# Adding the last expert layer's rows to the result in the scattering DMA, with the tiles beyond 28 in a branch

## The chip, the cores and the metric

The kernel runs on one core of one Trainium2 chip. The time is that of the device for one execution, in microseconds (us); lower is better. An execution was also recorded by the hardware profiler; its times are counted from the start of its span. PE is the matrix engine, DVE the vector engine, ACT the activation engine, POOL the GpSimd engine, SP the engine that issues most DMAs.

## The reference, cut to what matters

A graph network of two layers on 3125 nodes of 256 features. Each layer adds a graph convolution and an attention block to the stream `x`, then a mixture of experts. Only the last step, the experts of the second layer, matters here (`D` is 256, `H` 512, eight experts, two of them for each node):

```python
    mu = jnp.mean(x, axis=-1, keepdims=True)
    var = jnp.mean(jnp.square(x - mu), axis=-1, keepdims=True)
    xn = (x - mu) * jax.lax.rsqrt(var + EPS) * gamma + beta
    logits = jnp.einsum('bsd,de->bse', xn, Wr) + br
    top_vals, top_idx = jax.lax.top_k(logits, K)
    w = jax.nn.softmax(top_vals, axis=-1)
    w_full = jnp.einsum('bsk,bske->bse', w, jax.nn.one_hot(top_idx, E, dtype=w.dtype))
    y = jnp.zeros(x.shape[:-1] + (DOUT,), x.dtype)
    for e in range(E):
        h = jax.nn.gelu(jnp.einsum('bsd,dh->bsh', xn, W1[e]) + b1[e], approximate=False)
        y_e = jnp.einsum('bsh,hd->bsd', h, W2[e]) + b2[e]
        y = y + y_e * w_full[..., e, None]
    return y
```

The result is `x` plus this `y`: for each node, the stream before the step, plus two experts' outputs weighted by their gates.

## The kernel before

The stream lives in SBUF as `xs`, 25 tiles of 128 rows (the last of 53), and is worked on in seven groups of four tiles (the seventh is one tile). A framework orders the instructions of each engine and places semaphore waits where one instruction reads or overwrites what another wrote, in SBUF and in DRAM alike; `tc.declare_no_dep` takes such a wait away.

*Routing.* The second graph convolution ends in `sums` (L1271): for one group after another, PE multiplies the 25 row blocks of the adjacency matrix, loaded by SP as `chb` into four buffers, into PSUM. When a group is summed, `done2` (L1520) runs its two dense layers, adds to `xs` (L1543) and calls `route(g)` (L1197). The router normalizes the rows, chooses two experts for each node and gives each choice a place in the expert's list; POOL writes the row, with node number, first expert and both gates behind it, to that place of the DRAM array `slots` by an indirect DMA (L1242). Last, it adds the experts' second bias, weighted by the gates, to `xs` (L1254, L1255). SP's queue runs in order, so what stands in it between loads of `chb` is issued between them. The first five groups have passes of their own; the last two share one.

*The expert tiles.* An expert's list is cut into tiles of 256 rows. Their number depends on the data: at most NST = 32 for 6250 choices. A small table, computed on DVE, names list position and expert of each of the 32 tiles (L1562 to L1587). The loop at L1603 runs all 32, also where the lists fill fewer; the rest read blank rows. A tile: SP reads two numbers from the table and loads the expert's weights (`w1`, `w2`, 512 KB each, three buffers) and 256 rows (`xr`, 260 KB); PE transposes the rows (L190, evacuated at L192), multiplies them by `w1` (L224), ACT applies the gelu (L227), PE multiplies by `w2` (L1633) in two halves of 128 rows, DVE scales each half by its gate into `yo` (L1634, three buffers), and POOL scatters it by row into the DRAM array `y2_d` (L1635; the profile writes `y_d`). All these scatters are declared free of each other.

`y2_d` has a place for each node's first expert and, `HALF` = 3200 rows later, one for its second; rows of `xr` that hold no node go to places of their own behind, which nobody reads. So four operations on DVE make the destination `dest`:

```python
            V.tensor_scalar(second, xr[:, :, D + 1], te[:, i:i + 1], None, op0=OP.not_equal)
            V.scalar_tensor_tensor(unused, xr[:, :, D], float(2 * HALF), lost[:, i, :], op0=OP.is_ge, op1=OP.mult)
            V.tensor_tensor(unused, unused, xr[:, :, D], op=OP.add)
            V.scalar_tensor_tensor(dest, second, float(HALF), unused, op0=OP.mult, op1=OP.add)
```

*The end.* For each of the seven groups SP loads both halves of `y2_d` (L1648, L1651; 512 KB each, four buffers), DVE adds them to `xs` (L1653), and SP stores the group to `out` (L210, L212).

*Elsewhere.* Adding indirect DMAs (`compute_op=OP.add`, L384) build two count matrices in the first half of the kernel, one 4-byte value per partition. Two optional blocks, `residue`, stand in branches (`if_more`, L1324, entered at L1459 and L1514) that aren't entered with these inputs.

Of the kernel before, what the change touches and what calls it, by code (L numbers as in the profile page):

```python
# [8 lines left out]
F32 = mybir.dt.float32  # L9
BF16 = mybir.dt.bfloat16  # L10
I32 = mybir.dt.int32
AF = mybir.ActivationFunctionType
OP = mybir.AluOpType
# [4 lines left out]
P = 128  # L18
N = 3125
D = 256  # L20
NT = 25
NG = 7
LAST = N - 24 * P
NN = N * N
EX = 8
SLOT = 256
CAP = 13 * SLOT
NST = (2 * N + EX * (SLOT - 1)) // SLOT
XW = D + 4
HALF = 25 * P  # L30
E0 = 100000
E1 = 65536
MID = 13 * P
# [18 lines left out]
def rows_of(t):  # L52
    return P if t < NT - 1 else LAST


def tiles_of(g):
    return list(range(4 * g, min(4 * g + 4, NT)))
# [25 lines left out]
def tile_gps(ctx: ExitStack, tc: tile.TileContext, a, out):  # L83
    nc = tc.nc
# [45 lines left out]
    pq_d = dram.tile([9, N], F32, name="pq_d")  # L130
    y_d = dram.tile([NT, P, 4, D], F32, name="y_d")
    slots = dram.tile([EX * CAP + SLOT, XW], F32, name="slots")
    y2_d = dram.tile([3 * HALF + NST * SLOT + P, D], F32, name="y2_d")
    hT_d = dram.tile([P, 4, N], F32, name="hT_d")
    AT2 = AT[0:NN].rearrange("(r c) -> r c", c=N)
    A12 = A1[0:NN].rearrange("(r c) -> r c", c=N)
# [148 lines left out]
    def split_rows(r):  # L285

        return [(0, r)] if r % 16 == 0 else [(0, r - r % 16), (r - r % 16, r)]
# [152 lines left out]
    with ExitStack() as st:  # L440
# [74 lines left out]
        for g in range(NG):  # L515
            ts = tiles_of(g)
# [661 lines left out]
    def router(ps, moe):  # L1178
# [18 lines left out]
        def route(g):  # L1197

            ts = tiles_of(g)
            r, k = rows_of(ts[-1]), len(ts)  # L1200
            rb = moe.tile([P, 4, XW], F32, name="rb", tag="rb", bufs=2)
            nx = [rb[:r, j, :D] for j in range(k)]
            normed(nx, [xs[:r, t, :] for t in ts], r)
            normed(nx, nx, r)
            hT = work.tile([P, 2, 512], F32, name="hT", tag="hT")
            transposed(ps, hT, nx, r, [fcol("gamma", c) for c in range(2)], [fcol("beta", c) for c in range(2)], tag="mm", bufs=3)
            pl = ps.tile([P, 512], F32, name="mm", tag="mm", bufs=3)
            for j, t in enumerate(ts):
                for c in range(2):
                    T.matmul(pl[:r, EX * j:EX * j + EX], lhsT=hT[:, c, j * P:j * P + r], rhs=wr[:, c, :],  # L1210
                             start=(c == 0), stop=False)
                add_bias(pl[:r, EX * j:EX * j + EX], r, br)
            sc = moe.tile([P, 4, EX], F32, name="r_sc", tag="r_sc", bufs=2)
            V.tensor_copy(sc[:r, :k, :], pl[:r, :EX * k].rearrange("p (t e) -> p t e", e=EX))
            gt, rank = gates(moe, sc, EX, "r", nt=k, r=r, bufs=2)

            sel, pos, oh = (moe.tile([P, 4, EX], F32, name=f"r_{nm}", tag=f"r_{nm}", bufs=2)[:r, :k]
                            for nm in ("sel", "pos", "oh"))
            V.tensor_scalar(sel, rank, 1.5, None, op0=OP.is_lt)
            pp = ps.tile([P, 512], F32, name="mm", tag="mm", bufs=3)  # L1220
            sf = sel.rearrange("p t e -> p (t e)")
            T.matmul(pp[:r, :EX * k], lhsT=tri[:r, :r], rhs=sf, start=True, stop=True)
            T.matmul(pp[:, 64:64 + EX * k], lhsT=ones[:r, :], rhs=sf, start=True, stop=True)
            for j in range(k):
                V.tensor_tensor(pos[:, j, :], pp[:r, EX * j:EX * j + EX], nxt[:r], op=OP.add)
                V.tensor_tensor(nxt, nxt, pp[:, 64 + EX * j:64 + EX * j + EX], op=OP.add)
            at = moe.tile([P, 4, 2], F32, name="r_at", tag="r_at", bufs=2)
            ati = moe.tile([P, 4, 2], I32, name="r_ati", tag="r_ati", bufs=2)
            V.tensor_copy(rb[:r, :k, D], node[:r, ts[0]:ts[-1] + 1])
            for i in range(2):  # L1230
                V.tensor_scalar(oh, rank, float(i), None, op0=OP.is_equal)
                V.tensor_tensor(sel, oh, pos, op=OP.mult)
                V.tensor_reduce(at[:r, :k, i], sel, axis=AX.X, op=OP.add)
                V.tensor_tensor(sel, oh, gt, op=OP.mult)
                V.tensor_reduce(rb[:r, :k, D + 2 + i], sel, axis=AX.X, op=OP.add)  # L1235
                if i == 0:
                    V.tensor_tensor(sel, oh, ei[:r, None, :].to_broadcast([r, k, EX]), op=OP.mult)
                    V.tensor_reduce(rb[:r, :k, D + 1], sel, axis=AX.X, op=OP.add)
            V.tensor_copy(ati[:r, :k], at[:r, :k])
            for j in range(k):  # L1240
                for i in range(2):
                    d = G.indirect_dma_start(out=slots, out_offset=bass.IndirectOffsetOnAxis(ap=ati[:r, j, i:i + 1], axis=0),  # L1242
                                             in_=rb[:r, j, :], in_offset=None)
                    for o in spread:
                        tc.declare_no_dep(d.ins, o.ins, reason="every place is given once")
                    spread.append(d)

            for j, t in enumerate(ts):
                p = ps.tile([P, 512], F32, name="mm", tag="mm", bufs=3)
                T.transpose(p[:EX, :r], gt[:, j, :], ident[:r, :r])  # L1250
                gT = moe.tile([EX, P], F32, name="r_gT", tag="r_gT", bufs=2)
                S.activation(gT[:, :r], p[:EX, :r], AF.Copy)
                po = ps.tile([P, 512], F32, name="mm", tag="mm", bufs=3)
                T.matmul(po[:r, :D], lhsT=gT[:, :r], rhs=b2, start=True, stop=True)  # L1254
                V.tensor_tensor(xs[:r, t, :], xs[:r, t, :], po[:r, :D], op=OP.add)  # L1255

        return route

# [290 lines left out]
    with ExitStack() as st:  # L1549
# [3 lines left out]
        def stile(shape, name, dt=F32):  # L1553
            return fp.tile(shape, dt, name=name, tag=name)
# [39 lines left out]
        for h in range(4):  # L1594
            V.tensor_tensor(past, tmp, bb[:, h, :][:, None, :].to_broadcast([P, NST, EX]), op=OP.mult)
            V.tensor_reduce(b1[:, :, h], past, axis=AX.X, op=OP.add)


        lost = stile([P, NST, 2], "t_lost")
        G.iota(lost, pattern=[[SLOT, NST], [P, 2]], base=0, channel_multiplier=0, allow_small_or_imprecise_dtypes=True)  # L1600
        done = []
        why = "computed from counts, clamped above"
        for i in range(NST):  # L1603
            ro = nc.values_load(table[0:1, i, 0:1], engines=[mybir.EngineType.SP], min_val=0, max_val=EX * CAP,
                                skip_runtime_bounds_check_because=why)
            re = nc.values_load(table[0:1, i, 1:2], engines=[mybir.EngineType.SP], min_val=0, max_val=EX - 1,
# [7 lines left out]
            second = fp.tile([P, 2], F32, name="second", tag="second", bufs=3)  # L1614
            gate = fp.tile([P, 2], F32, name="gate", tag="gate", bufs=3)
            dest = fp.tile([P, 2], I32, name="dest", tag="dest", bufs=3)
            V.tensor_scalar(second, xr[:, :, D + 1], te[:, i:i + 1], None, op0=OP.not_equal)
            unused = fp.tile([P, 2], F32, name="unused", tag="unused", bufs=3)
            V.scalar_tensor_tensor(unused, xr[:, :, D], float(2 * HALF), lost[:, i, :], op0=OP.is_ge, op1=OP.mult)
            V.tensor_tensor(unused, unused, xr[:, :, D], op=OP.add)  # L1620
            V.scalar_tensor_tensor(dest, second, float(HALF), unused, op0=OP.mult, op1=OP.add)
            V.tensor_tensor(gate, xr[:, :, D + 3], xr[:, :, D + 2], op=OP.subtract)
            V.tensor_tensor(gate, gate, second, op=OP.mult)
            V.tensor_tensor(gate, gate, xr[:, :, D + 2], op=OP.add)
# [5 lines left out]
            for c in range(2):  # L1630
                po = ps.tile([P, D], F32, name="o", tag="o", bufs=3)
                for h in range(4):
                    T.matmul(po, lhsT=hid[h][:, c * P:(c + 1) * P], rhs=w2[:, h, :], start=(h == 0), stop=(h == 3))  # L1633
                V.tensor_scalar(yo[:, c, :], po, gate[:, c:c + 1], None, op0=OP.mult)  # L1634
                d = G.indirect_dma_start(out=y2_d, out_offset=bass.IndirectOffsetOnAxis(ap=dest[:, c:c + 1], axis=0),  # L1635
                                         in_=yo[:, c, :], in_offset=None)
                for o in done:
                    tc.declare_no_dep(d.ins, o.ins, reason="every result has a place; the dump is not read")
                done.append(d)

        for g in range(NG):
            ts = tiles_of(g)
            r = rows_of(ts[-1])
            for i in range(2):
                y = fp.tile([P, 4, D], F32, name="y2", tag="y2", bufs=4)
                at = HALF * i + 512 * g
                if len(ts) == 4:
                    nc.sync.dma_start(y, y2_d[at:at + 512, :].rearrange("(t p) d -> p t d", p=P))  # L1648
                else:
                    for q0, q1 in split_rows(r):  # L1650
                        nc.sync.dma_start(y[q0:q1, 0, :], y2_d[at + q0:at + q1, :])  # L1651
                xg = xs[:r, ts[0]:ts[-1] + 1, :]
                V.tensor_tensor(xg, xg, y[:r, :len(ts), :], op=OP.add)  # L1653
            store_rows(out, xs[:, ts[0]:ts[-1] + 1, :], g)


# [77 lines left out]
```

## Time and profile before

| | us |
|---|---|
| median of three runs | 5253.3 |
| the three runs | 5243.11, 5253.3, 5254.21 |
| the profiled execution | 5248.96 |
| span of its profile | 5247.1 |
| PE busy in the span | 4047.3 (77%) |
| DVE busy | 3311.5 (63%) |
| POOL busy | 2749.7 (52%) |
| ACT busy | 1361.2 (26%) |

The page cuts the span into 40 equal slices of 131 us; each digit is the busy share in tenths, 9 being 90% or more:

```profile
PE   0456878769666868859879946676799989999596
POOL 0568888888888888877740028788300120010121
DMA  9954543444322222266565554453543221121266
```

Up to slice 21 POOL is busy with the adding scatters of L384 nearly all the time; from slice 30 on, PE is. The expert stage is the last two slices and a little more. Its groups, from the answer by lines for 4600 to 5250 us (busy time, mean ns of one, idle time of the engine ahead of them and what ended it):

```profile
L224 PE MATMUL mm<-xT,f1w 128*128 128x256 f32 x512 | 127.8, 393 | 0.9 <-ACT xT L192 0.8
L1633 PE MATMUL o<-f1w,hid 128*128 128x256 f32 x512 | 115.7, 379 | 0.0
L1635 POOL DMA_INDIRECT y_d<-yo,dest x64 | 62.0, 968 | 199.1 <-DVE yo L1634 176.4 <-DVE gate L1622 22.5 <-issue 0.3
L1634 DVE TENSOR_SCALAR yo<-o,gate 128x256 f32<-128x256 f32 x64 | 30.9, 483 | 57.3 <-PE o L1633 56.5
L1653 DVE TENSOR_TENSOR xs<-xs,y 128x1024 f32<-128x1024 f32 (+1 forms) x14 | 15.5, 1109 | 22.0 <-DMA y<-y_d 22.0
```

### The profile page before, as it was taken

What the parts mean: (1) busy time and instruction counts of PE and PEld (TensorE: products, weight loads), DVE (VectorE), ACT (ScalarE), POOL (GpSimd) and SP (SyncE); (2) the same over time, 40 slices, a digit from 0 to 9 for tenths busy, and PEclk for the clock granted to TensorE, in tenths of its full rate; (3) what the DMA queues carried; (4) which work ended last, traced back from release to release, by engine and by line L of the source; (5) the groups of instructions that cost most, each with busy time, mean ns of one, the idle gap of its engine ahead of it and who ended that gap; (6) DMA issues with size and microseconds to landing.
All of it is one profiled execution on the core that took longest, in us unless ns stands there. A gap on an engine that the chain in (4) does not pass through costs nothing. (4 is left out here: it accounts for less than half of the span.)

```text
span 5247.1 us, 49144 instructions
## 1 busy us (share of the span) xinstructions
PE 4047.3 (77%) x16209; PEld 2337.5 (45%) x16277; DVE 3311.5 (63%) x8366; ACT 1361.2 (26%) x2089; POOL 2749.7 (52%) x1869
## 2 busy tenths in 40 slices
PE   0456878769666868859879946676799989999596
PEld 0244445445434554524456622232354444545485
DVE  7979887898799985123459978889860222321422
ACT  0111122113111211100025459898420120000132
POOL 0568888888888888877740028788300120010121
PEclk9867887889778878879989967688899999999798
DMA  9954543444322222266565554453543221121266
GB/s 355 332 131 72 83 63 53 78 79 61 25 17 25 25 17 8 5 137 128 89 184 203 180 142 124 116 140 93 182 126 89 65 80 52 53 59 39 68 210 191
DMA packets 462362, 548.06 MB, mean 104 GB/s; under 512 B 213429, under 2 KB 355550, under 8 KB 457049
## 3 DMA queue, kind: packets, MB, share of 16 engines
q1 hardware_dynamic: 266302, 509.57, 30.7%
q0 software_dynamic: 195792, 35.21, 13.1%
q8 instruction: 133, 2.18, 0.2%
q14 instruction: 135, 1.11, 0.1%
HBM read 412.74 MB, written 170.99 MB: 111 GB/s over the span
## 5 line engine op out<-in xcount | busy, mean ns | idle before, releaser
L384 POOL DMA_INDIRECT AT<-vala,keya x782 | 1237.6, 1583 | 439.9 <-issue 220.3
L384 POOL DMA_INDIRECT C<-valb,keyb x512 | 808.5, 1579 | 213.2 <-issue 144.0
L333 DVE SCALAR_TENSOR_TENSOR junk<-kr,keya,w_before 128x512 bf16<-128x512 f32 (+3 forms) x785 | 639.6, 852 | 10.7 <-DMA kr<-keys_a 8.8
L973 POOL TENSOR_TENSOR ex<-ex,pqb 128x1024 f32<-128x1024 f32 (+3 forms) x200 | 366.7, 1855 | 426.3 <-ACT ex L972 425.6
L190 PE MATMUL tr<-ident,rows 128*128 128x128 f32 (+1 forms) x500 | 102.3, 356 | 552.5 <-DVE rows L178 540.4
L373 DVE SCALAR_TENSOR_TENSOR junk<-kr,keyb,w_before 128x1024 bf16<-128x1024 f32 (+1 forms) x390 | 480.9, 1264 | 7.2 <-DMA kr<-keys_b 7.2
L1295 PE MATMUL ag<-chb,Hb 128*128 128x512 bf16 (+1 forms) x1753 | 414.7, 388 | 14.8 <-DMA chb<-A 12.8
L224 PE MATMUL mm<-hT,w 128*128 128x512 f32 (+1 forms) x896 | 407.7, 619 | 8.7 <-ACT hT L192 8.7
L872 DVE CUSTOM_DVE_ANT_0 am<-asb,pen 128x1664 f32<-128x1664 f32 (+3 forms) x200 | 357.2, 1786 | 55.4 <-ACT pen L869 45.4
L634 PE MATMUL o<-w,hid 128*128 128x256 f32 (+1 forms) x1600 | 383.2, 393 | 0.0
L1242 POOL DMA_INDIRECT slots<-rb,r_ati x50 | 49.7, 995 | 608.8 <-DVE rb L1235 595.7
L1008 PE MATMUL pa<-ex,hgp 128*32 128x512 f32 (+3 forms) x1400 | 224.6, 724 | 182.8 <-DVE ex L996 180.3
L996 DVE SCALAR_TENSOR_TENSOR ex<-ex,ct 128x2048 f32<-128x2048 f32 (+3 forms) x175 | 346.0, 2007 | 23.3 <-ACT ex L989 13.2
L192 ACT ACTIVATE hT<-tr,fm 128x512 f32<-128x512 f32 (+1 forms) x126 | 84.8, 720 | 1031.9 <-PE tr L190 1030.3
L989 ACT ACTIVATE ex<-ex,as 128x1024 f32<-128x1024 f32 (+3 forms) x400 | 345.3, 932 | 5.5 <-DVE ex L978 4.9
L190 PEld LDWEIGHTS tr<-ident,rows 128*128 128x128 f32 (+1 forms) x500 | 74.5, 174 | 584.3 <-issue 366.4
L634 PEld LDWEIGHTS o<-w,hid 128*128 128x128 f32 (+1 forms) x1600 | 297.1, 190 | 79.3 <-issue 38.6
L665 PE MATMUL ag<-ch,xn 128*128 128x512 f32 (+1 forms) x600 | 272.9, 603 | 55.0 <-DMA ch<-AT 55.0
L227 ACT ACTIVATE hid<-mm,fm 128x512 f32<-128x512 f32 (+1 forms) x336 | 211.3, 631 | 368.9 <-PE mm L224 363.5
L1295 PEld LDWEIGHTS <-Hb 128*128 128x128 bf16 (+1 forms) x2100 | 186.1, 99 | 228.7 <-issue 34.9
L224 PEld LDWEIGHTS mm<-hT,w 128*128 128x128 f32 x896 | 187.9, 228 | 220.2 <-issue 181.3
L660 DVE TENSOR_REDUCE most<-ch 128x1 f32<-128x1536 f32 (+3 forms) x50 | 89.0, 1780 | 219.2 <-DMA ch<-AT 219.1
(399 smaller groups left out, 6945.1 us busy)
## 6 DMA issues: line engine op xcount, KB each, us to landing
AT<-zero SPq DMA_DIRECT2D x25, 1528.0 KB
C<-zero SPq DMA_DIRECT2D x25, 1528.0 KB
cnt<-C SPq DMA_DIRECT2D x24, 1562.5 KB
cd<-C SPq DMA_DIRECT2D x36, 1024.0 KB
kr<-keys_b SPq DMA_DIRECT2D x64, 512.0 KB
f1w<-in_f_w_dram SPq DMA_DIRECT2D x64, 512.0 KB
kr<-keys_a SPq DMA_DIRECT2D x55, 512.0 KB
slots<-blank SPq DMA_DIRECT2D x15, 1820.0 KB
```

What stands on the lines that cost most here:

```text
L224: T.matmul(ph[:, :n], lhsT=w1[:, k, hb * P:(hb + 1) * P], rhs=xT[:, k, :n], start=(k == 0), stop=(k == 1))
L333: V.scalar_tensor_tensor(junk[:, :k * P], self.kr[:, at:at + k * P], key[:, c + j:c + j + 1], self.w_before[:, u:u + k * P], op0=OP.is_equ ...
L373: V.scalar_tensor_tensor(out, kk, key[:, c + j:c + j + 1], by, op0=OP.is_equal, op1=OP.mult, accum_out=more[:, j:j + 1] if i else self.val ...
L384: s = G.indirect_dma_start(out=self.flat, out_offset=bass.IndirectOffsetOnAxis(ap=self.idx[:, c:c + 1], axis=0), in_=self.val[:, c:c + 1], ...
L634: T.matmul(po[:r], lhsT=hid[hb][:, j * P:j * P + r], rhs=w2[:, hb, :], start=(hb == 0), stop=False)
L665: T.matmul(acc[fb, i][:, :n], lhsT=w, rhs=ch[:r, i * 512:i * 512 + n], start=s == 0 and (g != shared or fb == 0), stop=s == NT - 1 and (g ...
L872: V.tensor_tensor_reduce(out=junk[:r, :w], in0=asb[:r, h, c0:c1], in1=pen[:r, :w], scale=1.0, scalar=-3.0e38, op0=OP.subtract, op1=OP.max, ...
L973: G.tensor_tensor(e, e, pq[:r, h, :n], op=OP.add)
L989: S.activation(ex[:r, h, :n], ex[:r, h, :n], AF.Exp, bias=sc)
L996: V.scalar_tensor_tensor(e4, e4, 1.0, ct[:r, None, :m].to_broadcast([r, 4, m]), op0=OP.min, op1=OP.mult)
L1008: o = T.matmul(pa[32 * h:32 * h + 32, c:c + m], lhsT=hgp[:r, at:at + 32], rhs=ex[:r, h, c:c + m], start=(s == 0), stop=(s == NT - 1))
L1295: T.matmul(acc[fb, g][:, :n], lhsT=Xb[:r, s, i, fb * P:(fb + 1) * P], rhs=ch[:r, at:at + n], start=first, stop=last, skip_group_check=g == ...
```

## The change

The result is formed in DRAM. `route` stores each group of `xs` to `out` as soon as its bias is added, while the sums of the next groups run. Each expert tile's scatter then adds its rows to `out` in the DMA (`compute_op=OP.add`) with the node's number as destination; rows without a node have numbers from 6400 on and are left out by a bounds check. Within a tile the two halves are declared free of each other; between tiles the waits remain. `y2_d`, the loop over groups at the end and three DVE operations per tile are gone. The body of the loop becomes the function `expert_tile`; 28 tiles run always, the last four in a branch on the number of tiles, `total`, which is the last sum in the table's `cum`. The lines of the new file differ from the old ones by one up to L131 and by more behind.

```diff
+LIKELY = 28
...
-    y2_d = dram.tile([3 * HALF + NST * SLOT + P, D], F32, name="y2_d")
...
                 V.tensor_tensor(xs[:r, t, :], xs[:r, t, :], po[:r, :D], op=OP.add)
+            store_rows(out, xs[:, ts[0]:ts[-1] + 1, :], g)
...
-        lost = stile([P, NST, 2], "t_lost")
-        G.iota(lost, pattern=[[SLOT, NST], [P, 2]], base=0, channel_multiplier=0, allow_small_or_imprecise_dtypes=True)
-        done = []
+        total = stile([P, 1], "t_total", I32)
+        V.tensor_copy(total, cum[:, EX - 1:])
         why = "computed from counts, clamped above"
-        for i in range(NST):
+
+        def expert_tile(i):
+
...
+            V.tensor_copy(dest, xr[:, :, D])
             V.tensor_scalar(second, xr[:, :, D + 1], te[:, i:i + 1], None, op0=OP.not_equal)
-            unused = fp.tile([P, 2], F32, name="unused", tag="unused", bufs=3)
-            V.scalar_tensor_tensor(unused, xr[:, :, D], float(2 * HALF), lost[:, i, :], op0=OP.is_ge, op1=OP.mult)
-            V.tensor_tensor(unused, unused, xr[:, :, D], op=OP.add)
-            V.scalar_tensor_tensor(dest, second, float(HALF), unused, op0=OP.mult, op1=OP.add)
...
                 V.tensor_scalar(yo[:, c, :], po, gate[:, c:c + 1], None, op0=OP.mult)
-                d = G.indirect_dma_start(out=y2_d, out_offset=bass.IndirectOffsetOnAxis(ap=dest[:, c:c + 1], axis=0),
-                                         in_=yo[:, c, :], in_offset=None)
-                for o in done:
-                    tc.declare_no_dep(d.ins, o.ins, reason="every result has a place; the dump is not read")
-                done.append(d)
-
-        for g in range(NG):
...
-            for i in range(2):
-                y = fp.tile([P, 4, D], F32, name="y2", tag="y2", bufs=4)
-                at = HALF * i + 512 * g
...
-                V.tensor_tensor(xg, xg, y[:r, :len(ts), :], op=OP.add)
-            store_rows(out, xs[:, ts[0]:ts[-1] + 1, :], g)
+                d = G.indirect_dma_start(out=out, out_offset=bass.IndirectOffsetOnAxis(ap=dest[:, c:c + 1], axis=0),
+                                         in_=yo[:, c, :], in_offset=None, bounds_check=N - 1, oob_is_err=False,
+                                         compute_op=OP.add)
+                if c:
+                    tc.declare_no_dep(d.ins, before.ins, reason="a node has an expert once")
+                before = d
+
+        for i in range(LIKELY):
+            expert_tile(i)
+            if i == LIKELY - 5:
+                tiles = nc.values_load(total[0:1, 0:1], min_val=0, max_val=NST, skip_runtime_bounds_check_because=why)
+        with tc.If(tiles > LIKELY):
+            for i in range(LIKELY, NST):
+                expert_tile(i)
```

More of the change, by code (lines that the diff above doesn't have):

```diff
@@ L1634, in tile_gps @@
                 V.tensor_scalar(yo[:, c, :], po, gate[:, c:c + 1], None, op0=OP.mult)
-                d = G.indirect_dma_start(out=y2_d, out_offset=bass.IndirectOffsetOnAxis(ap=dest[:, c:c + 1], axis=0),
-                                         in_=yo[:, c, :], in_offset=None)
-                for o in done:
-                    tc.declare_no_dep(d.ins, o.ins, reason="every result has a place; the dump is not read")
-                done.append(d)
-        for g in range(NG):
-            ts = tiles_of(g)
-            r = rows_of(ts[-1])
-            for i in range(2):
-                y = fp.tile([P, 4, D], F32, name="y2", tag="y2", bufs=4)
-                at = HALF * i + 512 * g
[L1647 to L1652, printed above, removed]
-                V.tensor_tensor(xg, xg, y[:r, :len(ts), :], op=OP.add)
-            store_rows(out, xs[:, ts[0]:ts[-1] + 1, :], g)
+                d = G.indirect_dma_start(out=out, out_offset=bass.IndirectOffsetOnAxis(ap=dest[:, c:c + 1], axis=0),
[11 more added lines that the diff above has]
+                expert_tile(i)
 _OUT = ((N, D), "float32")
```

## The prediction, made before the changed kernel ran

> **What bounds the kernel now.** The change touches the last expert stage, so I first took busy time by stretches of 30 us, from the first tiles of that stage to the end of the span:
>
> ```profile
> core 0: us, PE busy (x) PEld busy (x) DVE busy (x) ACT busy (x) POOL busy (x), PEclk, DMA share, GB/s
> 4980.00:5010.00 30.00, 30.00 (x144) 25.20 (x143) 6.79 (x36) 11.33 (x24) 7.74 (x8) 1.00 0.66 205
> 5130.00:5160.00 30.00, 30.00 (x144) 25.24 (x143) 6.88 (x36) 11.36 (x24) 7.53 (x8) 1.00 0.66 209
> 5207.20:5247.10 39.90, 0.00 (x0) 0.00 (x0) 15.53 (x14) 0.00 (x0) 0.00 (x0) 0.51 0.78 241
> ```
>
> Two regimes. While tiles run, PE is busy 30.00 of 30.00 us at full clock, and DVE, ACT, POOL and the DMA engines have room. In the last 39.9 us PE, ACT and POOL do nothing and the DMA engines move 241 GB/s. Next, the timeline of POOL gives the period of a tile. Rows are start, duration, instruction, idle time before it and its releaser; the fourth pair from the end is the 28th tile, the last pair the 32nd:
>
> ```profile
> 5172.69 0.97 POOL L1635 DMA_INDIRECT y_d<-yo,dest  x1 [4.89 <-DVE yo L1634]
> 5174.41 0.97 POOL L1635 DMA_INDIRECT y_d<-yo,dest  x1 [0.76 <-DVE yo L1634]
> ...
> 5203.03 0.97 POOL L1635 DMA_INDIRECT y_d<-yo,dest  x1 [4.89 <-DVE yo L1634]
> 5204.76 0.97 POOL L1635 DMA_INDIRECT y_d<-yo,dest  x1 [0.76 <-DVE yo L1634]
> ```
>
> (5203.03 - 5172.69) / 4 = 7.585 us for a tile, and POOL waits for DVE, which waits for PE: a tile costs what PE needs. Third, the chain of work that ended last:
>
> ```profile
> 5204.76 2.40 DMA y_d<-yo,dest
> 5207.18 0.38 SPq L1648
> ...
> 5208.71 7.23 DMA y<-y_d
> ...
> 5218.88 7.68 DMA y<-y_d
> ...
> 5229.48 7.46 DMA y<-y_d
> ```
>
> After the last scatter has landed (5204.76 + 2.40 = 5207.16) the end is loads of y2 in batches of 7 to 8 us, with adds and stores between them: 5247.1 - 5207.16 = 39.9 us with nothing beside it. Last, three things that the change leans on: the landing time (from an instruction's start) of the plain scatter L1635, of the adding scatter L384 where the DMA engines were 0.71 busy (2280 to 2560 us), and a branch that is not entered (L1514) with POOL's drain at the end (L1730):
>
> ```profile
> DMA to landing us min/median/max: 2.4/3.9/4.6
> ```
>
> ```profile
> L384 POOL DMA_INDIRECT C<-valb,keyb x133: 1561/1564/2190, 2281.0 to 2558.9; - x133
> DMA to landing us min/median/max: 3.2/4.2/8.1
> ```
>
> ```profile
> L1514 PEldq COMPARE_BRANCH  x1: 3962/3962/3962, 4275.8 to 4275.8; - x1
> L1730 POOLq DRAIN  x3: 46/113/6958, 5204.5 to 5246.9; - x3
> ```
>
> **What the Trainium skill says.** "DMA: Bandwidth & Descriptors", Rules for kernel authors: an accumulating DMA reads its destination and writes it later, and a write that lands in between is lost, so it must wait for the earlier DMA's semaphore. Here that makes a chain of all tiles' scatters; the trace agrees in kind, as the adding scatters of L384 wait for landings of earlier ones (37.8 us of waits in those 280 us). "Collectives: The Full Stack", The bandwidth ceiling: an add in the DMA engines costs what its second source read costs, not the add. The trace can't show it for rows of 1 KB, as L384 adds single values. "Runtime: NRT & Kernel Launch", Instruction fetch mechanics: a taken branch out of the fetched window waits for its code. The trace agrees: 3.96 us on PE at L1514, 0.05 to 0.06 on the other engines.
>
> **Part 1, how many tiles run.** The branch is skipped if the experts fill at most 28 tiles. The profile cannot show the number, since before runs 32 whatever it is; I computed the reference's routing with its inputs. Its eight experts get 255, 1086, 1629, 2330, 149, 226, 432 and 143 rows, which is 1+5+7+10+1+1+2+1 = 28 tiles of 256. The margin is thin in one place: the expert with 255 rows must not reach 257. Skipped, four tiles at PE's pace go: 4 x 7.585 = -30.3 us. In the order of the changed kernel each engine loads the number and branches behind all of its work of tile 28; the loop isn't interrupted.
>
> **Part 2, the tail.** Gone are 12 loads of 512 KB and four small ones, 14 adds (15.5 us of DVE) and 7 stores, together the 39.9 us. What is late next is the landing of tile 28's second scatter. In before its first starts at 5172.69. An adding scatter held POOL 1.56 us, against 0.97 for the plain one; with the 0.30 us seen between neighbouring scatters the second starts at 5172.69 + 1.56 + 0.30 = 5174.55. It lands after 2.9 (least of all L384) to 4.2 us; no loads are left beside it, and I add 0.4 for rows of 1 KB: 3.3, so 5177.9. Then POOL's eight waits in the untaken branch (0.07 each, 0.5), and the closing barrier, which took 1.0 in before (last store landed 5246.1, end 5247.1): 5179.4. One thing may come later: POOL's drain ended at 5211.5 in before, 5.7 us after its last DMA instruction and hidden under the tail. Bare, it ends at 5176.1 + 5.7 = 5181.8, and the barrier at 5182.8. I take 5181, ends 5179.4 and 5182.8. PE's 4 us at the branch begin near 5174 and lie beside the landing. Against 5247.1 the sum is -66.1: the tiles -30.3, the tail 39.9 down to about 4.
>
> **Part 3, the stores moved to `route`.** Seven stores of `out` now stand in SP's queue among the loads of `chb` in the sums, each waiting for DVE's add L1255. Behind each wait loads that PE needs. In the new order the store of group 0 stands behind the tenth load of the next pass. In before's timeline the last L1255 of group 0 ends at 4405.47 and the eleventh load is issued at 4406.23 anyway; in the double pass the add ends at 4799.89 and the load behind it goes at 4800.07. So the stall is the store's own issue, 0.4 us, and four buffers (2.6 us of PE each) cover it: 0; uncovered, 6 x 0.4 = 2.4 us. The stores of groups 5 and 6 wait until 4935.8, while SP in before waits until 4949.2 for the table: 0.
>
> **Part 4, the scatter in the loop.** Tile i+1's first scatter now waits until both of tile i have landed; behind it on POOL stands only its own second half, and DVE's next-but-two `yo` waits for the buffer (three of them), then PE. The period of that chain is 1.86 (first to second start) + landing + some 0.15 to wake. With L384's median under load, 4.2, it is 6.2; rows of 1 KB add, at an estimated 40 to 100 ns for each of the 8 rows on an engine (a plain 4 KB packet of four rows took 159 ns in the trace), 0.3 to 0.8: 6.5 to 7.0. That is under 7.585, so PE stays the bound: 0. The landing may grow to 7.585 - 1.86 - 0.15 = 5.6 us first. DMA load is no bound: plain scatters hold 9.3% of the engines in this stage, and with double the reading the share goes from 0.66 to 0.75. The bounds check is nowhere in this trace. Below, it costs nothing, or even gains (rows out of range send nothing; scatter at the plain 0.97 would shorten the chain by 1.2); above, I can't exclude a microsecond or two of POOL. I take 0.
>
> **Part 5, small edits.** Three DVE operations of 0.16 us fewer per tile: DVE is 0.23 busy, 0. One copy for the number of tiles among the table's operations, up to 0.2 us ahead of the loop. An iota less on POOL, beside DVE's work: 0.
>
> **The sum.** 5247.1 - 66.1 = 5181 for the span, 5182.9 for that execution (5248.96, 1.86 around the span). The median of the three runs, 5253.3, lies 4.3 above the profiled execution; on its scale I forecast 5253.3 - 66 = 5187.
>
> **Rivals.**
> - *The chain of landings becomes the loop's bound.* For it: single landings of 8.1 us at a DMA share of 0.71, and only 0.6 to 1.1 us of room. Against it: median 4.2, three buffers to even it out, and a chain that slows also thins the loads it competes with. With a mean landing of 6.2 the period is 8.2, +0.6 x 27 = 17: about 5204.
> - *Slower: POOL's issue.* If the bounds-checked adding scatter is generated row by row on POOL, its duration d counts twice: period 2d + 3.8 (0.3 between, 0.15 to wake, 2.6 from POOL's end to landing at the median, 0.7 for the rows). It decides from d = 1.9 us; the whole gain is spent at 7.585 + 66/27 = 10.0, which is d = 3.1. At 3.5 the period is 10.8: 27 x 3.2 = +87, so 5274. For it: d already rose from 0.97 to 1.56 for adds. Against: the 1.56 hardly varies.
> - *The branch is entered,* the change doing only half of what it says: the chip's sums differ enough to make 29 tiles. Then the four tiles come back, with a cold start of about 10 us (PE's branch 4, first loads 5): 5187 + 40 = 5227. For it: 255 beside 256. Against: it takes two changed choices in one expert.
>
> **How the numbers follow.** Forecast 0.66, landing chain 0.22, branch entered 0.03, slow issue 0.09 (beyond break-even 0.06). The forecast's own range is 5178 to 5193: the ends of part 2, and the runs of before, which reach from 5243 to 5254. Landing chain and early slow issue fill up to 5210; beyond stand about 0.15. Range 5176 to 5210. About 0.2% (10.5 us) is what a measurement of this kernel can tell from no change. Faster 0.92; same 0.02 (slow issue near break-even); slower 0.06.
>
> **What would show it.** After: 56 scatters in place of 64, POOL about 1.56 us each; pairs 7.58 apart; PE busy 30.00 of 30.00 in the loop; no L1653; the end 5 to 8 us after the last scatter's start. Wrong, if pairs stand 8 us or more apart with PE idle before `o`, if 64 scatters ran, or if PE waits for `chb` in the sums.

## The result, and the profile after

| us | before | after |
|---|---|---|
| median | 5249.4 (5 runs, 5243.1 to 5254.2) | 5186.9 (5 runs, 5178.5 to 5209.3) |
| profiled execution | 5248.96 | 5178.45 |
| its span | 5247.1 | 5176.7 |
| first scatter of the expert stage | 4967.1 | 4961.4 |
| from there to the end of the span | 280.0 | 215.3 |

The ratio is 0.989, with a 95% interval from 0.9863 to 0.9917. The forecast was 5187. That it met the median almost exactly is partly chance: the medians differ by 62.5, where the forecast took off 66 from a median of three runs that lay higher. The two profiled spans differ by 70.4; the last row of the table, 64.7, is the part of it that belongs to the change. The other 5.7 arose ahead of the first scatter.

Busy time by stretches, two in the loop and the last from the last scatter's start to the end of the span:

```profile
core 0: us, PE busy (x) PEld busy (x) DVE busy (x) ACT busy (x) POOL busy (x), PEclk, DMA share, GB/s
4990.00:5020.00 30.00, 30.00 (x144) 25.16 (x144) 5.99 (x28) 11.68 (x24) 12.67 (x9) 1.00 0.77 202
5110.00:5140.00 30.00, 30.00 (x144) 25.18 (x143) 6.10 (x28) 11.34 (x24) 13.71 (x9) 1.00 0.78 196
5168.85:5176.70 7.85, 0.00 (x0) 0.00 (x0) 0.00 (x0) 0.00 (x0) 1.56 (x1) 0.69 0.18 20
```

PE is still busy 30.00 of 30.00 us. POOL's share has grown from 7.7 to about 13 us in 30, the DMA share from 0.66 to 0.77. After the last scatter 7.85 us remain where 42 us were.

POOL's timeline, its first pair and its 28th:

```profile
4961.43 1.65 POOL L1633 DMA_INDIRECT out_dram<-yo,dest  x1 [22.10 <-DVE gate L1620]
4963.38 1.58 POOL L1633 DMA_INDIRECT out_dram<-yo,dest  x1 [0.30 <-issue]
...
5166.98 1.56 POOL L1633 DMA_INDIRECT out_dram<-yo,dest  x1 [4.05 <-DVE yo L1632]
5168.85 1.56 POOL L1633 DMA_INDIRECT out_dram<-yo,dest  x1 [0.30 <-issue]
```

From the first to the 28th pair pass 5166.98 - 4961.43 = 205.55 us; before, 5172.69 - 4967.10 = 205.59. The loop runs at the same pace. The answer on the scatter's own line:

```profile
L1633 POOL DMA_INDIRECT out_dram<-yo,dest x56: 1562/1562/1652, 4961.4 to 5168.9; - x56
...
who waited for it (us, times):
  DVE dest L1618: 145.3, 25
...
DMA to landing us min/median/max: 2.7/4.5/5.6
```

There are 56 scatters, so the branch wasn't entered. The line to stop at is `DVE dest L1618`: DVE waits 25 times for a scatter to land, not at its own `yo` but at L1618, the copy into `dest`. The chain that ended last now runs through that wait:

```profile
5122.58 0.64 POOL out_dram L1633
5123.22 1.23 issue
5124.44 4.60 DMA out_dram<-yo,dest
5129.06 0.04 POOLq L1633
5129.11 1.21 issue
```

Before, the same view has no landing between the tiles:

```profile
5015.10 0.97 POOL y_d L1635
5016.06 4.66 issue
5020.95 0.97 POOL y_d L1635
```

There POOL went from one scatter to the next and waited for DVE's `yo`, which waited for PE. Now the chain alternates between a scatter, its landing, and 1.2 us called "issue", in which POOL waits for nothing that this view shows. DVE's and POOL's timeline of a neighbouring tile shows where those 1.2 us go:

```profile
5113.91 0.17 DVE L1618 CAST dest<-xr 128x2 int32<-128x2 f32 x1 [5.95 <-DMA out_dram<-yo,dest]
...
5114.51 0.16 DVE L1622 TENSOR_TENSOR gate<-gate,xr 128x2 f32<-128x2 f32 x1
5114.59 0.87 DVE L1632 TENSOR_SCALAR yo<-o,gate 128x256 f32<-128x256 f32 x2
5115.34 1.56 POOL L1633 DMA_INDIRECT out_dram<-yo,dest  x1 [4.05 <-DVE yo L1632]
5117.21 1.56 POOL L1633 DMA_INDIRECT out_dram<-yo,dest  x1 [0.30 <-issue]
```

`dest` has three buffers. On DVE, the `dest` of tile i+2 stands ahead of the `yo` of tile i, and it reuses the buffer from which tile i-1's scatters read their row numbers. So DVE sits until tile i-1 has landed, then does five small operations (the copy and four more) and only then the scaling that tile i's scatter needs. From landing to the next scatter's start pass 1.50 us (median of the 14 landings that the trace gives).

The end, from the answers on the branch's line and on the closing line:

```profile
L1644 PEldq COMPARE_BRANCH  x1: 423/423/423, 5166.5 to 5166.5; - x1
...
L1644 POOLq INC_SWDGE_SEM  x1: 897/897/897, 5172.0 to 5172.0; - x1
```

```profile
L1722 POOLq DRAIN  x3: 46/107/2972, 5172.9 to 5176.5; - x3
```

Behind the code of the branch, which isn't entered, POOL has a semaphore instruction of 0.90 us. It starts at 5172.0, when the last scatter has landed, 3.1 us after that scatter's start. Its drain starts at 5172.92, takes 2.97 us, and the barrier ends the span at 5176.7.

### The profile page after: what moved, and what is told of

It is laid out like the page before. It is cut to its first block, busy times and chain, and to the rows that moved or that the text cites. A ratio compares the mean times of both kernels' runs of the same rounds, so it can differ in the third digit from the quotient of the medians.

```text
span 5176.7 us, 48768 instructions
## 1 busy us (share of the span) xinstructions
PE 3988.3 (77%) x16133; PEld 2301.7 (44%) x16133; DVE 3286.6 (63%) x8261; ACT 1349.9 (26%) x2065; POOL 2778.6 (54%) x1860
## 5 line engine op out<-in xcount | busy, mean ns | idle before, releaser
L1296 PE MATMUL ag<-chb,Hb 128*128 128x512 bf16 (+1 forms) x1800 | 416.8, 386 | 12.2 <-DMA chb<-A 12.2
L996 DVE SCALAR_TENSOR_TENSOR ex<-ex,ct 128x2048 f32<-128x2048 f32 (+3 forms) x175 | 345.7, 2007 | 20.0 <-ACT ex L989 12.4
L1008 PE MATMUL pa<-ex,hgp 128*32 128x512 f32 (+3 forms) x1400 | 205.9, 668 | 196.5 <-DVE ex L996 193.9
```

The costliest lines, as they stand in the source:

```text
L996: V.scalar_tensor_tensor(e4, e4, 1.0, ct[:r, None, :m].to_broadcast([r, 4, m]), op0=OP.min, op1=OP.mult)
L1296: T.matmul(acc[fb, g][:, :n], lhsT=Xb[:r, s, i, fb * P:(fb + 1) * P], rhs=ch[:r, at:at + n], start=first, stop=last, skip_group_check=g == ...
```

## The experiments

Theory A: the gain is part 1 plus part 2, stores and scatter are hidden, and the chain of landings has no room left because of DVE's `dest`. Rival B: PE alone sets the loop, landings don't matter, and what spread the times have comes from the stages ahead of the experts; rival C: the adding scatter costs the loop something even where PE seems full.

**The changed kernel again, and with eight buffers for `dest`.** No edit in the first; in the second:

```diff
-            dest = fp.tile([P, 2], I32, name="dest", tag="dest", bufs=3)
+            dest = fp.tile([P, 2], I32, name="dest", tag="dest", bufs=8)
```

> The changed kernel once more, to stand beside the next three on the same chip. Its five runs so far reach from 5178 to 5209, those of before from 5243 to 5254. Theory A (landings level with PE): the wait for a tile's landing reaches DVE too, by the three buffers of dest, so the chain of tiles is 1.87 (both issues) + landing of the second half (4.2 on average in the profile) + about 1.4 (five small DVE operations, yo, wake) = 7.5 us, no shorter than PE's 7.585; a run with longer landings loses 27 us for each us. It expects 5180 to 5210 again, and in a profile of a slow run pairs of scatters over 7.7 us apart. Theory B (the stages ahead): the spread comes from the stages before the experts; then first to last pair is 205.5 us in any profile, and the same spread is seen in every kernel of this batch.

> dest has eight buffers in place of three, so DVE no longer waits for landings; POOL's own wait stays. Theory A: the chain is 1.87 + 4.2 + 0.2 = 6.3 us, well under PE's 7.585; the slow runs go, the median is 2 to 12 us lower than the unchanged kernel's (5175 to 5185), and DVE shows no waits for the scatter's landing. Theory B: the same median and the same spread as the unchanged kernel, within 3 us.

Beside a before of 5237.6, the changed kernel took 5180.0 (5168.4 to 5205.0), ratio 0.9893 (0.9874 to 0.9912), and eight buffers 5172.5 (5155.4 to 5175.9), ratio 0.9867 (0.9852 to 0.9882). The profiled execution of the unchanged copy happened to be one with a longer period: from its first to its 28th scatter 221.3 us, where 205.6 was seen above. Two of its windows, and three rows of its waits between 4960 and 5160 us (total, times, longest):

```profile
5080.00:5110.00 30.00, 26.25 (x122) 21.23 (x121) 5.88 (x28) 9.23 (x19) 10.21 (x7) 1.00 0.68 178
5110.00:5140.00 30.00, 25.09 (x118) 20.19 (x117) 4.41 (x21) 9.09 (x19) 10.61 (x8) 1.00 0.63 158
```

```profile
DVE dest L1618 <- DMA out_dram<-yo,dest: 114.5, 18, 8.0
...
DVE dest L1618 <- issue: 45.1, 6, 8.1
...
PE o L1631 <- DVE yo L1632: 9.8, 7, 1.8
```

The clock stands at 1.00, yet PE idles 8.7 us in 60, because it waits for DVE to empty the `o` banks, and DVE waits for landings. (The second row is of the same kind: the answer on the scatter's line counts 25 waits of `dest` for landings, 165.2 us in all.) The second halves landed after 5.00 us on the mean (13 seen), against 4.19 (14 seen) in the first profile of the changed kernel. 1.87 (first to second scatter) + 5.00 + 1.46 (landing to next start) = 8.33, and the mean period was 8.20; 1.87 + 4.19 + 1.51 = 7.57, and the period was 7.61. With eight buffers, the same waits view:

```profile
DVE dest L1618 <- DMA xr<-slots: 119.4, 24, 5.7
...
DVE yo L1632 <- PE o L1631: 30.7, 29, 5.4
```

DVE waits for `xr` and PE, not for landings; from landing to next scatter pass 0.81 us (median of 13), and the period is 7.61 with landings of 4.65. Its chain is then 1.87 + 4.65 + 0.81 = 7.33, with 0.28 us of room; by the same sum, an estimate, landings of 5.00 would make it 7.68 and not 8.2. So the wait and its cause are shown, and rival B falls for the loop. It keeps a part of the spread: the first scatter starts anywhere from 4948.7 to 4967.1 in the twelve traces of all kernels here. Why landings were longer in that one execution isn't shown.

**Does one more buffer do, and does it pay?** The same edit with `bufs=4`, beside the changed kernel a third time.

> The changed kernel with four buffers for dest instead of three: the smallest change that takes the copy into dest off the chain. With three, the dest of tile i+2 stands ahead of the yo of tile i on DVE and reuses the buffer of tile i-1, so it waits for that tile's last landing; with four it reuses that of tile i-2, which landed a period earlier. Theory: one more buffer is enough: no wait of DVE for a landing scatter, PE 30.00 of 30 in every window of the loop, period 7.61 to 7.62 in the profile, and a time as with eight (5172 where before is at 5237; ratio 0.986 to 0.988). Rival: it is the number of scatters in flight or the placing of buffers that helped with eight: then four leaves the waits or the spread of the changed kernel (ratio 0.989 or above).

> The changed kernel once more, beside the one with four dest buffers on the same chip. Theory: its runs lie higher and wider, since the chain of landings has no room: median 5 to 12 us above four buffers, single runs up to 30 above, none clearly below. Rival: no difference beyond 3 us, the earlier gap of 7.5 us being chance.

Four buffers: 5173.8 (5172.0 to 5177.0), ratio 0.9881 (0.9865 to 0.9898); DVE's waits for landings are gone and the period is 7.61. But the changed kernel took 5172.0 (5169.3 to 5178.0), ratio 0.988 (0.9864 to 0.9897): nothing between them, where 5 to 12 us had been expected. In its trace DVE waited 146.7 us for landings, as in the first profile, and PE was still busy 30.00 of 30.00 in each of six stretches from 4960 to 5140 us: the landings, 4.38 on the mean, stayed just short enough. So the extra buffer takes the wait off the chain. That it lowers the median, or does away with executions like the one above, is not shown: one comparison said 7.5 us, the next -1.8, and the kernel with four buffers was traced once.

**Plain scatter, nothing waits.** The experts' rows are scattered to `y2_d` as in before and are never added to `out`, which holds the stream alone; 28 tiles, branch and early stores as in the changed kernel, three `dest` buffers and the four operations that make `dest` as in before.

```diff
-                d = G.indirect_dma_start(out=out, ..., compute_op=OP.add)
+                d = G.indirect_dma_start(out=y2_d, ...)
+                for o in done:
+                    tc.declare_no_dep(d.ins, o.ins, reason="every result has a place; the dump is not read")
```

> Leaves out the adding of the experts' rows: the loop scatters as before, plainly, to places of its own in a DRAM array with no waits between scatters; the early stores, the 28 tiles and the branch are those of the changed kernel. What it is faster by is the whole price of the adding scatter in the loop and at the end. The prediction's step (price 0 in the loop, landing 0.9 later at the end): 1 to 2 us faster than the unchanged kernel's fastest runs. Theory A: 1 to 2 faster than the fastest, 5 to 15 faster in the median. A rival, that the adding itself loads the DMA engines and slows the weights: over 15 faster, with the DMA share of the loop at 0.66 against 0.78 to 0.84.

Measured: 5175.7 (5164.6 to 5179.7), ratio 0.988 (0.9865 to 0.9894), period 7.61. The answer on its scatter's line:

```profile
L1640 POOL DMA_INDIRECT y_d<-yo,dest x56: 967/971/1015, 4953.0 to 5160.3; - x56
...
DMA to landing us min/median/max: 2.4/3.8/5.2
```

The adding kernel with eight buffers is no slower than this one, so the adding costs the loop nothing that these runs can show: rival C falls for the loop. What it costs off the path is seen: POOL 1.56 for 0.97 us, landing 4.9 for 3.8, and a DMA share between 0.71 and 0.84 in the adding kernels, where PE is full, for 0.60 to 0.65. At the end it came out the other way than expected: the plain kernel's span ends 9.8 us after its last scatter's start, 2 us later than the changed kernel's, because POOL's drain took 5.09 us. Why it is longer there isn't shown.

**The second half waits for the first.** Doubling the suspected wait: landings now count twice in the chain.

```diff
-                if c:
-                    tc.declare_no_dep(d.ins, before.ins, reason="a node has an expert once")
-                before = d
```

> The second half's scatter waits for the landing of the first, too. If landings decide, as the prediction's rival has it, a tile costs 2 x landing (3.7 to 4.5) + 1.4 or so + wakes 0.3 = 9.1 to 10.7 us, so PE waits and the loop grows by 27 x (1.5 to 3.1) = 41 to 84 us: 5225 to 5270. If the landings were hidden deeper than I think (buffers take them up), less than 10 us are lost.

Measured: 5242.8 (5224.7 to 5252.1), ratio 1.0011 (1.0004 to 1.0018): the gain is gone. A tile's two scatters and the first of the next on POOL's timeline:

```profile
5143.85 1.56 POOL L1633 DMA_INDIRECT out_dram<-yo,dest  x1 [3.73 <-DVE yo L1632]
5148.32 1.56 POOL L1633 DMA_INDIRECT out_dram<-yo,dest  x1 [2.90 <-DMA out_dram<-yo,dest]
5155.32 1.56 POOL L1633 DMA_INDIRECT out_dram<-yo,dest  x1 [5.44 <-DVE yo L1632]
```

First to second start is now 4.62 on the mean; with the second landing (3.9) and 1.4 to the next start that is 9.9, and the mean period was 10.05. The loop is then 27 x (10.05 - 7.61) = 66 us longer; the medians of this kernel and the changed one differ by 62.8. "DMA: Bandwidth & Descriptors", Rules for kernel authors, in the Trainium skill asks for such a wait wherever two adding DMAs can meet in one place; here is its price, and the one line that declares the halves free is worth about the whole change.

**The two parts of the gain, each alone.** First, all 32 tiles always, without the branch, with eight `dest` buffers; second, the kernel before with its loop cut to 28.

```diff
-        for i in range(LIKELY):
+        for i in range(NST):
             expert_tile(i)
...
-        with tc.If(tiles > LIKELY):
-            for i in range(LIKELY, NST):
-                expert_tile(i)
```

```diff
-        for i in range(NST):
+        for i in range(28):
```

> Eight buffers for dest, and all 32 tiles always, without the branch; the last four tiles have blank rows alone, which the bounds check leaves out. By the prediction's part 1, four tiles cost 4 x 7.6 = 30 us, less up to 1 us for the branch that is gone: about 30 us above the kernel with eight buffers and 28 tiles (ratio to before 0.9867 + 0.0056 = 0.992 to 0.993), and about 36 us below before: that is the tail alone. Rival: if blank tiles were cheaper in the adding kernel (their scatters send nothing, so nothing lands late), or if the gain came from the tail alone, the ratio stays at 0.987 to 0.989. In the profile: 64 scatters, period 7.6, PE 30.00 of 30 through the four blank tiles too; the scatters of blank rows show what POOL pays for 128 rows that are all out of bounds (1.56 us if the descriptors are made anyway, less if not).

> The kernel before with its loop cut to 28 tiles, no branch; plain scatters, y2_d and the loads at the end stay. This is part 1 alone. Expected 4 x 7.585 = 30.3 us below before: ratio 0.9942. Rival: the last four tiles overlapped something that now stands bare (POOL's drain, 7 us, is under the tail either way; the tail's first loads could start no earlier), so that less than 20 us is gained: ratio above 0.996. Together with the run of 32 tiles the two parts should add up to the gain of 28 tiles with eight dest buffers, 65 to 70 us.

Beside a before of 5237.4: 32 tiles 5205.9 (5189.1 to 5209.0), ratio 0.9941 (0.9918 to 0.9964); before with 28 tiles 5211.6 (5194.2 to 5218.9), ratio 0.9947 (0.9927 to 0.9968). That is 31.5 and 25.8 us by the medians, a little under the 36 and 30 expected. They spread too much for a sum to the microsecond; the stretch from the first scatter's start to the end of the span, in which nothing else differs, does better:

| from first scatter to end, us | 32 tiles | 28 tiles |
|---|---|---|
| plain scatter, adds at the end | 280.0 | 249.5 |
| adding scatter | 244.1 (no branch, eight buffers) | 214.5 (no branch), 215.3 (branch) |

Downwards, 280.0 to 244.1 is part 2 alone: 35.9. Across, 280.0 to 249.5 is part 1 alone: 30.5. Together 66.4, and 280.0 - 214.5 = 65.5. A microsecond of this is noise: from first to 28th pair pass 206.6 and 206.5 us in the two adding kernels without a branch, 205.6 in the other three. Blank tiles are as dear as full ones: the last two pairs stand 5193.73 - 5186.14 = 7.59 us apart, and their scatters take as long:

```profile
L1633 POOL DMA_INDIRECT out_dram<-yo,dest x64: 1562/1562/1652, 4957.8 to 5195.6; - x64
```

The last eight of these 64 have all 128 rows out of bounds and still held POOL for 1.56 us each. They move no rows: after 5172 us POOL's DMA queue carried 0.01 MB.

**No early stores.** The seven groups of the stream are not written, so `out` gets the experts' rows alone.

```diff
-            store_rows(out, xs[:, ts[0]:ts[-1] + 1, :], g)
```

> The changed kernel without the stores in route: the seven groups of xs are not written, so out lacks the stream and gets the experts' rows alone. It tests part 3. Theory: the stores cost nothing, the time agrees with the changed kernel's within its own spread (5168 to 5209, ratio 0.987 to 0.991), and in the sums of the second convolution (4280 to 4960 us) PE's waits for chb are the same 12 us. Rival: the stores delay the loads of chb by 0.4 us each or more, and PE's waits for chb fall by 2.4 us or more; the time by as much, which only the profile can show.

Measured: 5171.2 (5165.9 to 5176.9), ratio 0.9882 (0.9861 to 0.9903), within the changed kernel's spread. In one stretch of the sums, at the same clock, first the changed kernel's windows row, then this one's:

```profile
4300.00:4500.00 200.00, 196.89 (x857) 97.32 (x856) 49.40 (x230) 10.99 (x22) 8.89 (x10) 0.99 0.19 53
```

```profile
4300.00:4500.00 200.00, 196.88 (x856) 97.21 (x855) 49.39 (x230) 10.97 (x22) 15.64 (x16) 0.99 0.19 55
```

PE idles 3.1 us of 200 with the stores and without them, 2.6 in the next 200 us either way, and its one wait for `chb` is 12.2 us with them and 12.4 without.

**No branch.** 28 tiles and nothing behind, so tiles beyond 28 would be left out; with these inputs there are none.

```diff
-        with tc.If(tiles > LIKELY):
-            for i in range(LIKELY, NST):
-                expert_tile(i)
```

> The changed kernel with 28 tiles in the loop and nothing behind: neither the number's loads nor the branch, so tiles beyond 28 would be left out (there are none with these inputs). It prices the branch and the end. Theory: the end after the last scatter's start stays 7 to 8 us, because POOL's drain waits for the last landing and takes about 3 us with or without a branch; the branch itself costs 0 to 1 us (POOL's semaphore instruction of 0.9 us). Rival: the drain's cost comes from the branch's reset of the DMA semaphores on POOL, and without it the end comes 5 us after the last scatter, 3 us earlier. The time cannot tell this from the changed kernel's spread; the profile's last 10 us do.

Measured: 5179.8 (5171.8 to 5191.6), ratio 0.9902 (0.9878 to 0.9926), no different by time. Its last scatter on POOL's timeline, and its closing line:

```profile
5163.86 1.56 POOL L1633 DMA_INDIRECT out_dram<-yo,dest  x1 [0.30 <-issue]
```

```profile
L1717 POOLq DRAIN  x3: 46/113/6637, 5162.6 to 5169.8; - x3
```

The long drain begins at 5162.6, while a scatter still runs, and ends at 5169.2, 5.4 us after the last scatter's start; the span ends at 5170.1, 6.2 after it, against 7.85 with the branch. Neither expectation had this right. In the kernel of 32 tiles, whose last scatters move no rows, the drain also ended 5.4 us after the last start. What it waits for there stays open. With the branch it cannot start before POOL has waited for the landing and spent 0.90 us on the semaphore instruction; it then needs 2.97 us of its own. The branch costs 1.6 us at the end.

## Why the prediction was right, point by point

*Part 1, four tiles less, -30.3:* right. The branch wasn't entered; the cut alone gave 30.5 in its trace.

*Part 2, the tail of 39.9 down to about 4:* right, 35.9 in the kernel without the branch. The end came 7.85 us after the last scatter's start, at the far end of "5 to 8" and later than the 6.45 taken. The last landing took 3.1 us where 3.3 was taken. That says little of rows of 1 KB: tile 28 holds 143 rows, so its second half has only 15 to add. The drain was named as what might come later, and it was what came last: it ended 5.5 us after POOL's last DMA instruction where 5.7 was put. That this fits is luck: without the branch it ended 3.8 us after it, and the term left out that behind the branch the drain starts only after the landing and the semaphore instruction. PE's 4 us at the branch were 0.42, and hidden either way.

*Part 3, the stores, 0:* right, by the run without them.

*Part 4, the scatter in the loop, 0:* right in its result, wrong in its margin. Three of its terms held: 1.87 for 1.86, a landing of 4.5 (median of all; 4.2 on the mean for the second halves, which the chain follows) where 4.2 + 0.3 to 0.8 was put, 1.56 us of POOL. The term "some 0.15 to wake" was mis-sized: POOL starts 0.8 us after a landing at best, and with three `dest` buffers 1.50. The step that failed is the list of who waits: it named the second half on POOL and DVE's `yo`, three buffers on, and passed over `dest`, which is also held by the scatter until it lands and whose next writer stands ahead of `yo` on DVE. So the landing may grow not to 5.6 but to 7.585 - 1.87 - 1.50 = 4.2, which is its mean. The DMA share was put at 0.75 and read 0.77 to 0.84, so the adding took more than the 0.09 of a second plain scatter. The term was mis-sized by the packets: between 4990 and 5140 us POOL's DMA queue held 9.3% of the engines before, with 1920 packets and 5.25 MB, and 23.0% after, with 5680 packets and 4.57 MB. The plain scatter moved four rows in a packet of 4 KB (159 ns at the median), the adding one a single row of 1 KB (102 ns).

*Part 5, small edits, 0:* nothing in the runs speaks against it; none tried it alone.

*The sum:* -66.1 for the span, against -64.7 in the stretch that it describes. By the medians, each beside its own before, the changed kernel gained 62.5, 57.6 and 61.2 us.

*The rivals.* "The chain of landings becomes the loop's bound" was put at 5204 with a mean landing of 6.2 and a period of 8.2. A single execution had the period of 8.2 already at 5.0, with PE idle before `o`: by the prediction's own sign of being wrong, this rival was true of it. The slowest runs, 5205 and 5209, reach that far, but they have no trace; the median doesn't. "Slow issue" is excluded: 1.56 us for every scatter, whether rows are in bounds or not. "The branch is entered" is excluded by 56 scatters.

## What to carry to other kernels

When a store is made into a read-modify-write that must wait for its predecessor, write the chain down as start to start + landing + all that stands between the landing and the next start, and look for every buffer that the DMA holds, its index list too: a three-deep buffer whose next writer stands early on an in-order engine joins the chain. Declare parts free of each other wherever the data allow it; here that one line is worth some 63 to 66 us. A change that removes work at the very end is priced by what then ends last, and behind an indirect DMA that includes POOL's drain.

## What the runs showed of the hardware that was not expected

- An indirect scatter on POOL takes 1.56 us with adding and bounds check, even with all 128 rows out of bounds, and 0.97 plain; in a kernel's 56 to 64 scatters no single one took over 0.1 us longer.
- The adding scatter went out in packets of one row (1 KB, 102 ns at the median), the plain one in packets of four rows (4 KB, 159 ns).
- From a landing seen by the trace to the start of the next waiting scatter pass 0.74 to 0.86 us where nothing else stands between.
- POOL's drain ended 5.4 us after the last adding scatter's start in two kernels without a branch; started after the landing, it still took 2.97 us with adding scatters, and 5.09 in the kernel with plain ones, where the end came 9.8 us after the last scatter's start.
- A branch over four tiles of code that wasn't entered held PE for 0.42 us (0.83 in one trace), the other engines for about 0.05.
